# x and w turned by VectorE in 32x32 blocks and placed by DMA, in a two-layer graph network

## The chip, the cores and the metric

The kernel runs on one core of a Trainium2 chip, as one program. The metric is the device time of one execution in microseconds. Five engines work side by side, each through its own queue in order: TensorE (PE in the profile, its weight loads PEld), VectorE (DVE), ScalarE (ACT), GpSimd (POOL) and SyncE (SP), which here only issues DMAs. An instruction starts when those before it on its engine are through and the semaphores that it waits for have been raised.

## The reference

64 graphs of 256 nodes with 256 features each. Cut to what matters:

```python
# layer 0, for all graphs; d = 256
xc = transpose(x, (0, 2, 1))
h = relu(bn1(conv1d(xc, conv1_w, 0)))                # width 1
h = bn2(conv1d(h, conv2_w, 8))                       # width 17
x_conv = transpose(relu(h + xc), (0, 2, 1))
s = x @ w_se.T + b_se                                # 3 numbers a node
A = exp(-dist(s)) * adj
msg = relu(x @ w_msg.T + b_msg)
x_nmp = einsum('bnm,bmd->bnd', A, msg)
gi = concatenate([x_conv, x_nmp], -1) @ w_ih.T + b_ih
gh = x @ w_hh.T + b_hh
r, z = sigmoid(gi_r + gh_r), sigmoid(gi_z + gh_z)
out0 = (1 - z) * tanh(gi_n + r * gh_n) + z * x
x = layernorm(x + out0)
# layer 1
h = layernorm(x)
agg = einsum('bij,bjh->bih', adj, h)
x = layernorm(x + x + relu(agg @ W_rel + b_rel + h @ W_root))
```

The inputs besides `x` and `adj` are weights, biases and batch-norm statistics. All is float32.

## The kernel before

Features lie on partitions in layer 0 (a node's features run down the partitions, in C = 2 halves of 128), nodes lie on partitions in layer 1. So x has to be turned once at the start, and the result of layer 0, called w (twice the sum of x and the layer's output), once in the middle.

**Batches and pairs.** The width-17 convolution works on batches of 8 graphs (`conv`, 8 batches b = 0 to 7), all else on pairs of two graphs (`pair`, 32 pairs p = 0 to 31, four to a batch). The convolution is computed as products of polynomials: `split`, `merge` and `butterflies` are VectorE work on the tile XF, `products` has TensorE's matmuls with the transformed filters. These filters are computed once, stored to DRAM (w2m), and for batches after the first loaded in portions into the two halves of the tile cs (`load_w`, 768 KB each, two portions in flight). `conv1(b)` prepares a batch: for each two graphs it loads x (`fetch`), turns it by eight TensorE transposes through PSUM and two ScalarE copies into xTc (`turned`), stores xTc to DRAM (xt), multiplies by the width-1 filter and stores the result (hd), which the convolution loads later into XF. `pair(p)` loads xT from xt again.

**A pair** goes through: msg and the three numbers of s (`ps_msg`), the distances (`ps_sT`, `ps_dist`), A (AT times adjm), nmp; the sum of convolution and x (xc); the gates. For pairs 2 to 30 the gate products are done in seven instead of eight block products: differences of blocks are formed by VectorE in tx (of xT), tn (of nmp) and tc (of xc), and `product` multiplies them by sums of weight blocks in WB. A gate's sums leave the PSUM banks `ps_a`, `ps_b`, `ps_d` by `put` (ScalarE, into RG for r and the hidden part, into ZN for z and n) and `onto` (VectorE). Then five VectorE operations over 1024 columns and a tanh make w in the tile wT, features on partitions.

**norm, project, aggregate.** `norm` turns w: eight TensorE transposes per pair into two PSUM banks (`ps_wT`). For pairs 0 to 27 ScalarE copies each half of a bank to x1 and sums it on the way (`total`), then squares it with the mean taken off (into the part of HY that is free then), GpSimd makes the factors q and the shifts sh from the sums, and ScalarE normalizes x1 in place. For the last four pairs (`late`) VectorE takes the statistics directly from PSUM. `project` multiplies wT with both weight matrices of layer 1 (`ps_hy`), scales by q into HY; `aggregate` multiplies by the adjacency (`ps_agg`), adds, takes the maximum with zero and adds x1, sums, normalizes and stores to out.

**The order** is not the order of the code. Every operation is recorded with a due time (`prog.at(when, step)`; a pair's due is 143.0 + 60.5 p us, GATE_TIME is the planned length of a gate) and planned costs (`dur`, for a DMA 0.06 us on SyncE's queue and its bytes at 205 GB/s after 1.6 us), and `scheduled` builds each engine's queue from these, taking of the operations that are ready the one with the earliest due time. `prog.group()` makes one planned operation of several instructions. The built program keeps this order on each engine whatever the real times are. The eight PSUM banks are given out by the planner, at most 4 to the gates, 3 to the convolution, 6 to the rest. All DMAs but three small ones at the start (ScalarE's) go through SyncE's queue; in the built program they use eight semaphores in turn, so a DMA also waits for the one issued eight before it.

Of the kernel before, what the change touches and what calls it, by code (L numbers as in the profile page):

```python
# [15 lines left out]
AF = mybir.ActivationFunctionType  # L16
ALU = mybir.AluOpType

P = 128
# [31 lines left out]
LEAVES += [(U + 2, U + 3, PI / 2)]  # L51
NM = 3 * len(LEAVES) + 2
SR, LR = 32, 100
OB = 7
HQ = 2 * M * C * (M + 1)
XC_SLOTS = BG + 2
FIRST_GATES, PERIOD, GATE_TIME = 143.0, 60.5, 18.0
AHEAD_FROM, AHEAD_TO, W_DEEP = -20.0, 10.0, 2
CONV1_FROM, CONV1_TO, CONV_FROM, CONV_OUT, CONV_TO = -10.0, 120.0, -6.0, -70.0, -30.0
PAIR_LEAD, FILTER_LEAD, LOAD_AHEAD = 20.0, 15.0, 12.0  # L60
PLAIN, SUMS_FROM = (0, 1, B // 2 - 1), 2


# [199 lines left out]
class Engine:  # L263
# [4 lines left out]
    def __getattr__(self, method):  # L268
        program, name = self.program, self.name

        def call(*args, hold=(), need=(), lines_up=0, **named):
            line = sys._getframe(1 + lines_up).f_lineno
            outs = [v for v in (named.get("out"), named.get("accum_out"), named.get("out_")) if v is not None]
            outs += [] if "out" in named else [args[0]]
            ins = [v for v in list(args) + list(named.values()) if not any(v is o for o in outs)]
            if method == "matmul" and not named.get("start", True):
                ins.append(outs[0])

            def places(vs):
                return [v if isinstance(v, View) else dram_cells(v) for v in vs  # L280
                        if isinstance(v, View) or hasattr(v, "tensor")]
            n = max((v.size() for v in outs if isinstance(v, View)), default=0)
            moved = 0
            if method == "dma_start":
                v = outs[0] if isinstance(outs[0], View) else named["in_"]
                dur, moved = 0.06, v.size() * v.at.shape[0] * 4
            elif name == "tensor":
                turned = method == "transpose" or named.get("is_transpose")
                dur = 0.109 if turned else 2 * max(0.109, n * 0.8333e-3 + 0.0025)
            elif name == "vector":  # L290
                dur = 0.182 if method == "bn_aggr" else 0.147 + 1.044e-3 * (args[1].size() if method == "bn_stats" else n)
# [114 lines left out]
def gnn_two_layers(  # L406
# [373 lines left out]
    def conv1(b):  # L780
# [3 lines left out]
        XN = {}  # L784

        def fetch(g):
            if b > 0:
                XN[g] = xn_ahead[:, :4 * D].rearrange("p (j d) -> p j d", d=D)
            elif g >= 4:
# [4 lines left out]

        def turned(g):
            xn = XN[g]
            if b > 0 or g == 4:
                xTc = xTc_ahead
            elif g:
# [39 lines left out]
    def conv(b):  # L839
# [8 lines left out]
        if b == 0:  # L848
            run(other)
        sv, s8, s4 = {}, {}, {}  # L850
        todo = [(lambda k=k: products(b, 2 * k, S + 2 * k), merges(0, k, S, sv, b == 0)) for k in range(4)]
        todo += [(lambda k=k: products(b, 8 + 2 * k, S2 + 2 * k), merges(1, k, S2, s8, b == 0)) for k in range(2)]
        todo += [(lambda: products(b, 12, S2 + 4), merges(2, 0, S2 + 4, s4, b == 0)), (lambda: last_products(b), None)]
        vector = deque([other])
        share, spent = 61.0 / len(todo), 0.0
        for i, (make, after) in enumerate(todo):
# [80 lines left out]
    bhh = sb("bhh", [P, 3, C])  # L937
    half_r = sb("half_r", [P, C])
    half_z = sb("half_z", [P, C])
    sts = sb("sts", [P, 3 * LR + P])  # L940
    sts.base.fine = 0
    lr = sb("lr", [P, 2, N])
    prog.at(22.0, 0.001)
# [28 lines left out]
    store_w2(1)  # L972

    xTs = [sb(f"xT{i}", [P, C, 2, N], "ahead") for i in range(2)]
    msg = sb("msg", [P, 2, C, D], "ahead")
    AT = sb("AT", [P, 2, C, N], "ahead")
    adjm = sb("adjm", [P, 2, C, N], "ahead")
    nmp = sb("nmp", [P, C, 2, N], "ahead")

    first = conv(0)  # L980
    at4 = len(prog.ops)
# [3 lines left out]
    opened["work"] = first_closed  # L985
    WB = sb("WB", [P, 7, 3, 3, P], "work")
    tx = sb("tx", [P, 4, N], "work")
    tn = sb("tn", [P, 3, N], "work")
    tc_ = sb("tc", [P, 3, N], "work")
    RG = sb("RG", [P, 4, 2, N], "work")  # L990
    ZN = sb("ZN", [P, 4, 2, N], "work")
# [58 lines left out]
    def pair(p):  # L1050
# [10 lines left out]
        at = p % 2 * C * LR  # L1061
        st = sts[:, at:at + C * LR].rearrange("p (m e) -> p m e", m=C)

        def spot(m, g):
            o = at + m * LR + 2 * g * SR
            return sts[:, o:o + 2 * SR].rearrange("p (r e) -> p r e", r=2)[:, :, 0:3]
        idle = p < 2
        for g in range(2):
            for m in range(C):
# [5 lines left out]
                    if idle:  # L1075
                        PE.matmul(ps[:, :D + 4], ones[0:1, :], bms[0:1, :], start=False, stop=True)
                if idle:
                    A.copy(spot(m, g), ps[:, D:D + 3].unsqueeze(1).to_broadcast([P, 2, 3]))
                    A.activation(msg[:, g, m], ps[:, :D], AF.Relu)
                    continue  # L1080
                V.tensor_add(spot(m, g), ps[:, D:D + 3].unsqueeze(1).to_broadcast([P, 2, 3]),
                             bms[:, D:D + 3].unsqueeze(1).to_broadcast([P, 2, 3]))
                V.tensor_add(msg[:, g, m], ps[:, :D], bms[:, :D])
            if not idle:
                A.activation(msg[:, g], msg[:, g], AF.Relu)
        sq, ns = next(sqs), next(nss)
        s = st[:, :, :3 * SR].rearrange("p m (r e) -> p m r e", e=SR)[:, :, ::2, 0:3]
        G.tensor_mul(sq, s, s)
# [39 lines left out]
        A.activation(xc, xc, AF.Relu)  # L1128
        ins = (xT, nmp, xc)
        right = []  # L1130
        for v, t, when in zip(ins, (tx, tn, tc_), (due - 28, due - 10, due - 20)):
# [5 lines left out]
            t1, t2, t4 = (t[:, i, :] for i in range(3))  # L1137
            t3 = t[:, 3, :] if v is xT else b12
            V.tensor_sub(t1, b12, b11)
            V.tensor_sub(t2, b22, t1)  # L1140
            V.tensor_sub(t4, b21, t2)
            V.tensor_sub(t3, b22, b12)
            right.append((b11, b21, b22, t4, t1, t2, t3))

        def product(ps, i, second, start):
# [94 lines left out]
        def norm(gs):  # L1240
# [2 lines left out]
            js = slice(2 * gs[0], 2 * gs[-1] + 2)  # L1243
            total, squares, mv = next(totals), next(totals), next(mvs)
            source = {}
            for g in gs:
                ps = bank("ps_wT")
                with prog.group():
                    for m in range(C):
# [14 lines left out]
            else:  # L1264
# [4 lines left out]
            G.tensor_scalar(q[:, 0, js], var, part, 4 * EPS, ALU.mult, ALU.add)  # L1269
            G.tensor_scalar(q[:, 1, js], var, (1 + EPS) * part, 4 * EPS * EPS, ALU.mult, ALU.add)  # L1270
            G.tensor_tensor(q[:, :, js], q[:, :, js], mhalf.rearrange("p (a c) -> p a c", a=2)[:, :, js], ALU.pow)
            G.tensor_mul(sh[:, js], mean, q[:, 0, js])
            if late:
                G.tensor_scalar(sh[:, js], sh[:, js], -1.0, None, ALU.mult)
            for g, m, j in spots(gs):
                A.activation(x1[:, g, m, :], source[j], AF.Identity, bias=sh[:, j:j + 1], scale=q[:, 0, j:j + 1])
            return q

        def project(gs, q):
            prog.at(due + 2 * GATE_TIME + 8, 0.6)  # L1280
            for g, m, j in spots(gs):
                ps = bank("ps_hy")
                with prog.group():
                    for f in range(C):
                        PE.matmul(ps, wT[:, 2 * f + g, m * P:(m + 1) * P], wrr[:, f, :], start=(f == 0),  # L1285
                                  stop=(f == C - 1), hold=[HY[:, g, m]], need=[q[:, 1, j:j + 1]])
                stt(HY[:, g, m, :], ps, q[:, 1, j:j + 1], hrow)  # L1287

        def aggregate(gs):
            prog.at(due + 2 * GATE_TIME + 16, 0.4)  # L1290
            q, sh = next(q3s), next(shs)
            js = slice(2 * gs[0], 2 * gs[-1] + 2)
            total, squares, mv = next(totals), next(totals), next(mvs)
            for g in gs:
# [5 lines left out]
                                      start=(m == 0), stop=(m == C - 1))  # L1300
                y = HY[:, g, :, D:]
                V.tensor_add(y, y, ps.rearrange("p (m d) -> p m d", m=C))
                if late:
                    stt(y, y, 0.0, x1[:, g], op0=ALU.max, op1=ALU.add)
                for m in range(C):
                    j = 2 * g + m
                    if late:
                        stats(mv[:, j, :], y[:, m, :])
                    else:
                        V.scalar_tensor_tensor(y[:, m, :], y[:, m, :], 0.0, x1[:, g, m], op0=ALU.max, op1=ALU.add,  # L1310
                                               accum_out=total[:, j:j + 1])
            if late:
                mean, var, part = mv[:, js, 0], mv[:, js, 1], 1.0
            else:
# [5 lines left out]
            G.tensor_scalar(q[:, js], var, part, EPS / 4, ALU.mult, ALU.add)  # L1320
            G.tensor_tensor(q[:, js], q[:, js], mhalf[:, js], ALU.pow)
            G.tensor_mul(sh[:, js], mean, q[:, js])
            if late:
                G.tensor_scalar(sh[:, js], sh[:, js], -1.0, None, ALU.mult)
            for g in gs:
                y = HY[:, g, :, D:]
                for m in range(C):
# [120 lines left out]
```

## Time and profile before

| | us |
|---|---|
| median of 3 runs | 2087.59 |
| lowest, highest | 2084.59, 2087.82 |
| profiled execution | 2085.32 |
| span of the profiled execution (first to last instruction) | 2083.5 |
| mean granted TensorE clock | 0.994 |
| DMA queue of SyncE: packets, MB, share of the span of 16 engines | 207518, 238.92, 35.6% |

Busy time by stage, from stretches of the same execution:

| stretch, us | what | PE busy | DVE busy | ACT busy | DMA share |
|---|---|---|---|---|---|
| 143 to 385 | pairs 0 to 3 | 238.48 | 181.93 | 106.44 | 0.43 |
| 627 to 869 | four pairs in the middle | 241.75 | 206.60 | 123.16 | 0.37 |
| 1353 to 1595 | four pairs later | 241.83 | 207.54 | 121.15 | 0.36 |
| 1900 to 2020 | pairs without convolution beside them | 117.96 | 71.09 | 53.40 | 0.13 |
| 2060 to 2084 | the end | 10.91 | 9.11 | 3.09 | 0.06 |

From 143 us on the pairs follow each other about 60 us apart, and TensorE is busy nearly all of it. The profile counts matmuls in records: a product of float32 is two records, a transpose one. The page's part on DMA issues gives the median time from issue to landing:

```profile
cs<-w2m SPq DMA_DIRECT2D x105, 768.0 KB, 4.8
adjm<-in_adjT_dram SPq DMA_DIRECT2D x64, 256.0 KB, 2.8
xT<-xt SPq DMA_DIRECT2D x32, 512.0 KB, 3.7
out_dram<-HY SPq DMA_DIRECT2D x64, 256.0 KB, 2.1
```

SyncE's own operations carry the time that the engine needs to issue a DMA, without its transfer.

### The profile page before, as it was taken

How to read it: one execution, taken by the hardware profiler on the slowest of the kernel's cores; microseconds unless marked ns; L12 is line 12 of the kernel's file. 1: busy time of each engine (PE TensorE's matmuls, PEld its weight loads, DVE VectorE, ACT ScalarE, POOL GpSimd, SP SyncE). 2: the span in 40 equal slices, each digit the busy share in tenths (PEclk: the TensorE clock that was granted, in tenths of full speed). 3: DMA queues.
4: the chain of work that ended last, by engine and by line, in shares of the span. 5: the costliest groups of instructions: out<-in, count | busy, mean ns of one | idle time of the engine just before them, and what ended most of it. 6: DMA issues, size and time to landing. Idle time of an engine off the chain costs nothing.

```text
span 2083.5 us, 28847 instructions
## 1 busy us (share of the span) xinstructions
PE 2048.0 (98%) x10492; PEld 1664.2 (80%) x10492; DVE 1685.8 (81%) x3028; ACT 1018.1 (49%) x2216; POOL 317.2 (15%) x555
## 2 busy tenths in 40 slices
PE   9989999999999999999999999999999999999996
PEld 6868779778887788878888788877888779887775
DVE  7983898899868998789868998689887899875644
ACT  7443433754447544564436544464445544365432
POOL 4100210122111201111101121112011220011101
PEclk9989999999999999999999999999999999999999
DMA  7734363334423244224433245232442225211100
GB/s 211 262 98 144 124 208 112 118 102 141 161 81 120 92 160 141 94 92 141 165 107 113 72 139 170 96 112 91 159 138 83 76 74 161 75 50 53 41 21 31
DMA packets 208201, 241.19 MB, mean 116 GB/s; under 512 B 23749, under 2 KB 192700, under 8 KB 208060
## 3 DMA queue, kind: packets, MB, share of 16 engines
q1 hardware_dynamic: 207518, 238.92, 35.6%
q8 instruction: 83, 1.36, 0.3%
q14 instruction: 58, 0.48, 0.1%
q10 hardware_dynamic: 542, 0.43, 0.1%
HBM read 177.85 MB, written 61.47 MB: 115 GB/s over the span
## 4 chain that ended last, share of the span: by engine, by line
PE 94%; DVE 4%; issue 1%; ACT 0%; POOL 0%; ACTq 0%; POOLq 0%; DVEq 0%
PE ps_a L1155 21%; PE ps_k L703 16%; PE ps_d L1155 11%; PE ps_hy L1285 11%; PE ps_msg L1073 5%; PE ps_agg L1299 5%; PE ps_c L828 5%; PE ps_b L1155 5%; PE ps_g L1155 5%; PE ps_nmp L1121 4%; PE ps_w L561 2%; PE ps_wT L1252 1%; PE ps_xTc L807 1%; PE ps_dist L1107 1%; DVE RG L1230 1%
## 5 line engine op out<-in xcount | busy, mean ns | idle before, releaser
L703 PEld LDWEIGHTS ps_k<-XF,cs 128*128 128x128 f32 x2632 | 313.2, 192 | 13.0 <-issue 6.6
L703 PE MATMUL ps_k<-XF,cs 128*128 128x128 f32 x2632 | 315.4, 275 | 0.0
L1285 PE MATMUL ps_hy<-wrr,wT 128*128 128x512 f32 x512 | 226.8, 595 | 0.0
L1285 PEld LDWEIGHTS ps_hy<-wrr,wT 128*128 128x128 f32 x512 | 96.6, 191 | 107.0 <-issue 102.1
L1169 ACT ACTIVATE RG<-ps_a,bhh 128x512 f32<-128x512 f32 x116 | 79.5, 686 | 191.0 <-PE ps_a L1155 129.4
L1155 PE MATMUL ps_a<-tx,WB 128*128 128x256 f32 x522 | 156.7, 382 | 0.0
L1167 ACT COPY ZN<-ps_a 128x512 f32<-128x512 f32 x116 | 67.6, 583 | 156.5 <-PE ps_a L1155 156.2
L1287 DVE SCALAR_TENSOR_TENSOR HY<-ps_hy,q,hrow 128x512 f32<-128x512 f32 x128 | 95.8, 749 | 55.8 <-PE ps_hy L1285 41.1
L675 DVE TENSOR_TENSOR XF<-XF 128x512 f32<-128x512 f32 (+3 forms) x128 | 126.4, 1010 | 5.3 <-ACT XF L756 3.0
L1073 PE MATMUL ps_msg<-wms,xT 128*128 128x260 f32 x512 | 124.7, 384 | 0.0
L1299 PE MATMUL ps_agg<-HY,adja 128*128 128x256 f32 x512 | 119.1, 380 | 4.0 <-issue 3.5
L1121 PE MATMUL ps_nmp<-AT,msg 128*128 128x256 f32 x512 | 118.8, 380 | 3.0 <-DVE AT L1114 3.0
L1299 PEld LDWEIGHTS ps_agg<-HY,adja 128*128 128x128 f32 x512 | 96.3, 190 | 31.3 <-issue 16.1
L1073 PEld LDWEIGHTS ps_msg<-wms,xT 128*128 128x128 f32 x512 | 95.3, 190 | 19.1 <-issue 5.8
L1121 PEld LDWEIGHTS ps_nmp<-AT,msg 128*128 128x128 f32 x512 | 95.4, 190 | 18.8 <-DVE AT L1114 4.2
L828 PE MATMUL ps_c<-xTc,w 128*128 128x512 f32 x232 | 107.7, 594 | 0.5 <-ACT xTc L808 0.5
L1155 PEld LDWEIGHTS ps_a<-tx,WB 128*128 128x128 f32 x522 | 95.1, 191 | 14.0 <-issue 1.5
L1155 PE MATMUL ps_a<-tc,WB 128*128 128x256 f32 x348 | 103.8, 380 | 0.0
L1155 PE MATMUL ps_a<-xc,WB 128*128 128x256 f32 x348 | 103.6, 379 | 0.0
L1155 PE MATMUL ps_a<-tn,WB 128*128 128x256 f32 x348 | 103.5, 379 | 0.0
L1155 PE MATMUL ps_a<-nmp,WB 128*128 128x256 f32 x348 | 103.5, 379 | 0.0
L1265 POOL TENSOR_SCALAR total<-total 128x4 f32<-128x4 f32 x28 | 15.5, 552 | 544.9 <-ACT x L1261 544.9
(213 smaller groups left out, 4642.7 us busy)
## 6 DMA issues: line engine op xcount, KB each, us to landing
cs<-w2m SPq DMA_DIRECT2D x105, 768.0 KB, 4.8
adjm<-in_adjT_dram SPq DMA_DIRECT2D x64, 256.0 KB, 2.8
xT<-xt SPq DMA_DIRECT2D x32, 512.0 KB, 3.7
adja<-in_adjT_dram SPq DMA_DIRECT2D x64, 256.0 KB, 2.7
out_dram<-HY SPq DMA_DIRECT2D x64, 256.0 KB, 2.1
hd<-xn SPq DMA_DIRECT2D x28, 544.0 KB, 3.2
XF<-hd SPq DMA_DIRECT2D x28, 544.0 KB, 4.0
xt<-xTc SPq DMA_DIRECT2D x29, 512.0 KB, 4.0
```

The lines of the kernel that those rows point to most:

```text
L561: PE.matmul(ps[:, :NM * OB], TT[i][:, a, :], taps, start=True, stop=True)
L675: (V.tensor_add if add else V.tensor_sub)(sl(o, n), sl(a, n), sl(b, n))
L703: PE.matmul(ps[:, o * P:(o + 1) * P], w(m, c)[:, o * P:(o + 1) * P], X[:, slot, c * P:(c + 1) * P], start=first and o == 0 and c == 0, sto ...
L828: PE.matmul(ps, w1[:, c, o * P:(o + 1) * P], xTc[:, c, :], start=(c == 0), stop=(c == C - 1), hold=[h[:, :, o]])
L1073: PE.matmul(ps[:, :D + 4], xT[:, c, g, m * P:(m + 1) * P], wms[:, c, :], start=(c == 0), stop=(c == C - 1 and not idle), hold=[msg[:, g, m]])
L1121: PE.matmul(ps[:, d * N:(d + 1) * N], msg[:, g, m, d * P:(d + 1) * P], AT[:, g, m, :], start=(m == 0), stop=(m == C - 1), hold=[nmp[:, :, g]])
L1155: PE.matmul(ps[:, h * N:(h + 1) * N], block[:, s, gate, :], right[s][at], start=start and h == 0 and j == 0, stop=j == len(sources) - 1, s ...
L1167: A.copy(o, ps)
L1169: A.activation(o, ps, AF.Identity, bias=bhh[:, 2, f:f + 1])
L1285: PE.matmul(ps, wT[:, 2 * f + g, m * P:(m + 1) * P], wrr[:, f, :], start=(f == 0), stop=(f == C - 1), hold=[HY[:, g, m]], need=[q[:, 1, j: ...
L1287: stt(HY[:, g, m, :], ps, q[:, 1, j:j + 1], hrow)
L1299: PE.matmul(ps[:, n_ * D:(n_ + 1) * D], adja[:, g, m, n_ * P:(n_ + 1) * P], HY[:, g, m, :D], start=(m == 0), stop=(m == C - 1))
```

## The change

For batches 3 to 7 (`TURN_FROM`) x is loaded in runs of 32 floats by 16 DMAs for two graphs, each to 32 partitions, so that 32x32 blocks lie where their turned ones belong; one VectorE operation turns all blocks into xTc. For pairs 2 to 27 (`W_FROM`, not `late`) w is turned likewise: VectorE turns the blocks of wT into the part of ZN that n has left free, and 32 DMAs of 128 runs of 128 bytes carry the blocks to their places in x1, where ScalarE sums them (into the scratch part of HY). The transposes of TensorE and the evictions from PSUM for these are gone. `project` and `aggregate` of these pairs are due 15 us later (`W_LAG`); the planner counts the bytes of grouped DMAs 2.5 times (`SMALL_RUNS`).

Small operations are joined: the bias is added to msg and s at once over 260 columns, and s is copied to its places by ScalarE; the differences for tx and for nmp (whose tile now holds the differences too, tn is gone) partly two at once; `merge` joint in every batch; in `aggregate` the maximum and sum with x1 for both halves at once, with the sums taken by ScalarE. For late pairs some small operations on statistics go from GpSimd to VectorE, and a multiplication by -1 is joined. In the last pair the products of `project` no longer wait for q.

```diff
-FIRST_GATES, PERIOD, GATE_TIME = 143.0, 60.5, 18.0
+FIRST_GATES, PERIOD, GATE_TIME = 143.0, 60.5, 17.0
+SMALL_RUNS, TURN_FROM = 2.5, 3
+W_FROM, W_LAG = 2, 15.0
...
                 dur, moved = 0.06, v.size() * v.at.shape[0] * 4
+                if program.joined is not None:
+                    moved *= SMALL_RUNS
...
         def fetch(g):
+            if b >= TURN_FROM:
+                XN[g] = xn_ahead[:, :4 * D]
+                blocks = XN[g].rearrange("p (c g b i) -> p g c b i", c=C, g=2, i=SQ)
+                with prog.group():
+                    for a in range(P // SQ):
+                        for k in range(2):
+                            for c in range(C):
+                                at = c * P + a * SQ
+                                SP.dma_start(out=blocks[a * SQ:(a + 1) * SQ, k, c], in_=x[b * BG + g + k][
+                                    :, at:at + SQ].rearrange("(b j) i -> j b i", j=SQ))
+                return
...
         def turned(g):
             xn = XN[g]
+            if b >= TURN_FROM:
+                V.transpose(xTc_ahead.rearrange("p c n -> p (c n)"), xn)
+                SP.dma_start(out=xt_dram[(b * BG + g) // 2], in_=xTc_ahead)
+                return xTc_ahead
...
                 if idle:
-                    A.copy(spot(m, g), ps[:, D:D + 3].unsqueeze(1).to_broadcast([P, 2, 3]))
-                    A.activation(msg[:, g, m], ps[:, :D], AF.Relu)
+                    A.copy(msg[:, g, m], ps[:, :D + 4])
                     continue
-                V.tensor_add(spot(m, g), ps[:, D:D + 3].unsqueeze(1).to_broadcast([P, 2, 3]),
-                             bms[:, D:D + 3].unsqueeze(1).to_broadcast([P, 2, 3]))
-                V.tensor_add(msg[:, g, m], ps[:, :D], bms[:, :D])
-            if not idle:
-                A.activation(msg[:, g], msg[:, g], AF.Relu)
+                V.tensor_add(msg[:, g, m], ps[:, :D + 4], bms)
+        for m in range(C):
+            A.copy(places(m), msg[:, :, m, D:D + 3].unsqueeze(2).to_broadcast([P, 2, 2, 3]))
+        for g in range(2):
+            A.activation(msg[:, g, :, :D], msg[:, g, :, :D], AF.Relu)
...
-            for g in gs:
+            if not late and p >= W_FROM:
+                blocks = ZN[:, :, 1, :]
+                V.transpose(blocks.rearrange("p j (c n) -> p j c n", c=C),
+                            wT.rearrange("p (c g) (m n) -> p (g m) c n", c=C, m=C))
+                with prog.group():
+                    for a in range(P // SQ):
+                        for b in range(P // SQ):
+                            for c in range(C):
+                                SP.dma_start(
+                                    out=x1[b * SQ:(b + 1) * SQ].rearrange("j g m d -> j (g m) d")[
+                                        :, :, c * P + a * SQ:c * P + (a + 1) * SQ],
+                                    in_=blocks[a * SQ:(a + 1) * SQ, :, c * P + b * SQ:c * P + (b + 1) * SQ])
+                for g, m, j in spots(gs):
+                    source[j] = x1[:, g, m, :]
+                    A.activation(HY[:, g, m, :D], x1[:, g, m, :], AF.Copy, accum_out=total[:, j:j + 1])
+            for g in gs if late or p < W_FROM else ():
...
-            prog.at(due + 2 * GATE_TIME + 8, 0.6)
+            prog.at(due + 2 * GATE_TIME + 8 + (0.0 if late or p < W_FROM else W_LAG), 0.6)
...
-                                  stop=(f == C - 1), hold=[HY[:, g, m]], need=[q[:, 1, j:j + 1]])
+                                  stop=(f == C - 1), hold=[HY[:, g, m]], need=[] if apart else [q[:, 1, j:j + 1]])
...
-                if late:
-                    stt(y, y, 0.0, x1[:, g], op0=ALU.max, op1=ALU.add)
+                stt(y, y, 0.0, x1[:, g], op0=ALU.max, op1=ALU.add)
...
-                        V.scalar_tensor_tensor(y[:, m, :], y[:, m, :], 0.0, x1[:, g, m], op0=ALU.max, op1=ALU.add,
-                                               accum_out=total[:, j:j + 1])
+                        A.activation(HY[:, g, m, :D], y[:, m, :], AF.Copy, accum_out=total[:, j:j + 1])
```

More of the change, by code (lines that the diff above doesn't have):

```diff
@@ L53 @@
 SR, LR = 32, 100
+SQ = 32
 OB = 7
@@ L850, in conv @@
         sv, s8, s4 = {}, {}, {}
-        todo = [(lambda k=k: products(b, 2 * k, S + 2 * k), merges(0, k, S, sv, b == 0)) for k in range(4)]
-        todo += [(lambda k=k: products(b, 8 + 2 * k, S2 + 2 * k), merges(1, k, S2, s8, b == 0)) for k in range(2)]
-        todo += [(lambda: products(b, 12, S2 + 4), merges(2, 0, S2 + 4, s4, b == 0)), (lambda: last_products(b), None)]
+        todo = [(lambda k=k: products(b, 2 * k, S + 2 * k), merges(0, k, S, sv, True)) for k in range(4)]
+        todo += [(lambda k=k: products(b, 8 + 2 * k, S2 + 2 * k), merges(1, k, S2, s8, True)) for k in range(2)]
+        todo += [(lambda: products(b, 12, S2 + 4), merges(2, 0, S2 + 4, s4, True)), (lambda: last_products(b), None)]
         vector = deque([other])
@@ L939, in gnn_two_layers @@
     half_z = sb("half_z", [P, C])
-    sts = sb("sts", [P, 3 * LR + P])
+    sts = sb("sts", [P, LR + P + 4])
     sts.base.fine = 0
@@ L974, in gnn_two_layers @@
     xTs = [sb(f"xT{i}", [P, C, 2, N], "ahead") for i in range(2)]
-    msg = sb("msg", [P, 2, C, D], "ahead")
+    msg = sb("msg", [P, 2, C, D + 4], "ahead")
     AT = sb("AT", [P, 2, C, N], "ahead")
     adjm = sb("adjm", [P, 2, C, N], "ahead")
-    nmp = sb("nmp", [P, C, 2, N], "ahead")
+    nmps = sb("nmp", [P, 7, N], "ahead")
+    nmp = nmps[:, 1:5].rearrange("p (c g) n -> p c g n", c=C)
     first = conv(0)
@@ L987, in gnn_two_layers @@
     tx = sb("tx", [P, 4, N], "work")
-    tn = sb("tn", [P, 3, N], "work")
     tc_ = sb("tc", [P, 3, N], "work")
@@ L1060, in pair, with places @@
         prog.at(due - 62, 0.6)
-        at = p % 2 * C * LR
+        at = p % 2 * 4
         st = sts[:, at:at + C * LR].rearrange("p (m e) -> p m e", m=C)
-        def spot(m, g):
-            o = at + m * LR + 2 * g * SR
-            return sts[:, o:o + 2 * SR].rearrange("p (r e) -> p r e", r=2)[:, :, 0:3]
+        def places(m):
+            o = at + m * LR
+            return sts[:, o:o + 4 * SR].rearrange("p (g r e) -> p g r e", g=2, r=2)[:, :, :, 0:3]
         idle = p < 2
@@ L1130, in pair @@
         right = []
-        for v, t, when in zip(ins, (tx, tn, tc_), (due - 28, due - 10, due - 20)):
+        for v, t, when in zip(ins, (tx, nmps, tc_), (due - 28, due - 10, due - 20)):
             prog.at(when, 0.3)
@@ L1136, in pair @@
                 continue
-            t1, t2, t4 = (t[:, i, :] for i in range(3))
+            t1, t2, t4 = (t[:, i, :] for i in ((0, 5, 6) if v is nmp else range(3)))
             t3 = t[:, 3, :] if v is xT else b12
-            V.tensor_sub(t1, b12, b11)
+            if v is xT:
+                V.tensor_sub(t[:, 0::3], v[:, :, 1, :], v[:, 0])
+            elif v is nmp:
+                V.tensor_sub(t[:, 0:3:2], t[:, 2:5:2], t[:, 1:3])
+            else:
+                V.tensor_sub(t1, b12, b11)
             V.tensor_sub(t2, b22, t1)
             V.tensor_sub(t4, b21, t2)
-            V.tensor_sub(t3, b22, b12)
+            if v is xc:
+                V.tensor_sub(t3, b22, b12)
             right.append((b11, b21, b22, t4, t1, t2, t3))
@@ L1268, in norm @@
                 mean, var, part = total[:, js], squares[:, js], 1.0 / D
-            G.tensor_scalar(q[:, 0, js], var, part, 4 * EPS, ALU.mult, ALU.add)
-            G.tensor_scalar(q[:, 1, js], var, (1 + EPS) * part, 4 * EPS * EPS, ALU.mult, ALU.add)
+            small = V if late else G
+            small.tensor_scalar(q[:, 0, js], var, part, 4 * EPS, ALU.mult, ALU.add)
+            small.tensor_scalar(q[:, 1, js], var, (1 + EPS) * part, 4 * EPS * EPS, ALU.mult, ALU.add)
             G.tensor_tensor(q[:, :, js], q[:, :, js], mhalf.rearrange("p (a c) -> p a c", a=2)[:, :, js], ALU.pow)
-            G.tensor_mul(sh[:, js], mean, q[:, 0, js])
             if late:
-                G.tensor_scalar(sh[:, js], sh[:, js], -1.0, None, ALU.mult)
+                stt(sh[:, js], mean, -1.0, q[:, 0, js], op1=ALU.mult)
+            else:
+                G.tensor_mul(sh[:, js], mean, q[:, 0, js])
             for g, m, j in spots(gs):
@@ L1285, in project @@
                         PE.matmul(ps, wT[:, 2 * f + g, m * P:(m + 1) * P], wrr[:, f, :], start=(f == 0),
-                                  stop=(f == C - 1), hold=[HY[:, g, m]], need=[q[:, 1, j:j + 1]])
+                                  stop=(f == C - 1), hold=[HY[:, g, m]], need=[] if apart else [q[:, 1, j:j + 1]])
                 stt(HY[:, g, m, :], ps, q[:, 1, j:j + 1], hrow)
         def aggregate(gs):
-            prog.at(due + 2 * GATE_TIME + 16, 0.4)
+            prog.at(due + 2 * GATE_TIME + 16 + (0.0 if late or p < W_FROM else W_LAG), 0.4)
             q, sh = next(q3s), next(shs)
@@ L1319, in aggregate @@
                 mean, var, part = total[:, js], squares[:, js], 1.0 / D
-            G.tensor_scalar(q[:, js], var, part, EPS / 4, ALU.mult, ALU.add)
+            (V if late else G).tensor_scalar(q[:, js], var, part, EPS / 4, ALU.mult, ALU.add)
             G.tensor_tensor(q[:, js], q[:, js], mhalf[:, js], ALU.pow)
-            G.tensor_mul(sh[:, js], mean, q[:, js])
             if late:
-                G.tensor_scalar(sh[:, js], sh[:, js], -1.0, None, ALU.mult)
+                stt(sh[:, js], mean, -1.0, q[:, js], op1=ALU.mult)
+            else:
+                G.tensor_mul(sh[:, js], mean, q[:, js])
             for g in gs:
```

## The prediction

> **What bounds the kernel now.** I read the page's engine table first, then the groups by shape, then TensorE's timeline, then SyncE's own timeline. Columns of a group: line, engine, operation, tiles, shape, count | busy us, mean ns | idle before it.
>
> ```profile
> PE 2048.0 (98%) x10492; PEld 1664.2 (80%) x10492; DVE 1685.8 (81%) x3028; ACT 1018.1 (49%) x2216; POOL 317.2 (15%) x555
> PE 94%; DVE 4%; issue 1%; ACT 0%; POOL 0%; ACTq 0%; POOLq 0%; DVEq 0%
> L1252 PE MATMUL ps_wT<-ident,wT 128*128 128x128 f32 x256 | 35.5, 281 | 10.4 <-DVE wT L1231 10.4
> L807 PE MATMUL ps_xTc<-ident,xn 128*128 128x128 f32 x224 | 31.8, 273 | 0.0
> L1231 DVE SCALAR_TENSOR_TENSOR wT<-ZN,RG 128x1024 f32<-128x1024 f32 x28 | 34.3, 1225 | 1.0
> ```
>
> TensorE is busy 98% of the span and 94% of the chain of waits, so a TensorE instruction taken away is worth its pace, as long as nothing makes TensorE wait. The pace is the distance of starts in its timeline (start, length, engine, line, count), since the 273 ns of one matmul include an overlapped tail:
>
> ```profile
> 609.26 1.06 PE L1252 MATMUL ps_wT<-ident,wT 128*128 128x128 f32 x8 [0.17 <-DVE wT L1231]
> 610.16 0.60 PE L807 MATMUL ps_xTc<-ident,xn 128*128 128x128 f32 x4
> 610.60 0.60 PE L1155 MATMUL ps_d<-tx,WB 128*128 128x256 f32 x2
> 611.03 0.59 PE L1155 MATMUL ps_d<-tc,WB 128*128 128x256 f32 x2
> ```
>
> Eight transposes take 0.90 us: 0.112 us each. One 256-column product (two records) takes 0.43.
>
> **What comes off.** The built order of the changed kernel has 5203 TensorE instructions instead of 5571: 26 pairs x 8 of w and 5 batches x 4 x 8 of x, 368 in all. 368 x 0.112 = 41 us. In the last pair, four small GpSimd operations on statistics go to VectorE and two of them are dropped (rows of 0.31 to 0.46 us against 0.15 or so); this chain stands bare at the end, about -2 us. Gain in sight: 43 us.
>
> **VectorE and ScalarE.** 46 block turns of 128x1024 come to VectorE. No row shows one; I take 1.22 us, the row of any other 1024-element operation there (L1231); between half and twice that, the chain below moves by -0.6 to +1.2 us. Against 46 x 1.22 = 56 us stand the joined operations: 120 spot additions (L1081, 161 ns) and 112 half-size sums with accumulation (L1310, 423 + 82 ns, now 56 of some 0.69 us) leave, two merges or subtractions become one. Counted out with the rows by size, VectorE's total stays within 10 us. ScalarE gets 112 sums (0.49 us each), loses 40 evictions (0.587): about +50 us on 49%. Neither is near a bound; both are priced nothing on the path, and the cover is their idle time.
>
> **The DMAs, which are the price.** w is no longer evicted from PSUM: 32 DMAs of 16 KB per pair bring the blocks from ZN to x1, and 16 per two graphs bring x. All go through SyncE's one queue. Its rows (a small transfer each in the first fence; the second has two in a row in mid-kernel):
>
> ```profile
> 24.64 0.43 SPq L956 DMA_DIRECT2D hrow<-in_rows_dram  x1
> 25.12 0.43 SPq L957 DMA_DIRECT2D gb<-in_rows_dram  x1
> 25.59 0.51 SPq L958 DMA_DIRECT2D bih<-in_rows_dram  x1
> ```
>
> ```profile
> 142.28 0.39 SPq L793 DMA_DIRECT2D xn<-in_x_dram  x1
> 142.73 0.49 SPq L842 DMA_DIRECT2D XF<-hd  x1
> ```
>
> The issue takes about the same for 2 KB (gb) as for 544 KB (XF): 0.34 to 0.54, and starts lie 0.45 to 0.48 apart. The shortest row is 0.319 (XF, min of 28). I take 0.45; ends 0.33 and 0.54. A train of 32 is then 14.4 us, with 16 of x 21.6. The planner in the kernel counts 0.06 an issue and, with the new factor of 2.5 on bytes, 6.4 + 1.6 = 8.0 us to the landing. I take the landing of the last at 2.1 (least row: out_dram): 16.5 in place of 8.0, so every train lands 8.5 us later than the order of all engines was laid out for.
>
> Could the transfer itself be slower than its issue? Two stretches (the last two columns are the DMA engines' busy share and GB/s):
>
> ```profile
> 60.00:100.00 40.00, 40.00 (x277) 34.69 (x275) 36.69 (x57) 16.81 (x38) 1.87 (x1) 1.00 0.83 274
> 131.00:133.00 2.00, 2.00 (x10) 1.26 (x11) 2.00 (x4) 0.75 (x4) 0.12 (x1) 1.00 0.92 267
> ```
>
> In the second the 512-byte runs of WB load: 512 / (267 / 0.92 / 16) = 28 ns a packet. A train has 4096 / 16 = 256 packets an engine: 7 us at that price, below 14.4. The trend to the 1 KB packets of the first (w2m; 1024 / (274 / 0.83 / 16) = 50 ns) would make 128 bytes about 13 ns, 3 us. So issue decides.
>
> The Trainium skill speaks against the change here: "DMA: Bandwidth & Descriptors", Specifications, says that below 512 bytes a transfer costs a read-modify-write. Taken as two passes of the 28 ns row, an estimate by that page would be 56 ns a packet and 14.3 us a train, equal to the issue; no row here shows 128-byte runs. The same page (Issuing engines are not separate DMA queues) calls the time to initiate a DMA usually small beside the DMA; the rows above show 0.4 us beside 16 KB, where it is the larger part.
>
> **Where the lateness arrives.** From the last gate product of a pair to the end of the wait: onto 0.69, two updates 2.44, two tanh 1.44, three updates 3.66, turn 1.22 = 9.45; train and landing 16.5; then ScalarE, in order, reads x1 four times (4 x 0.49 = 2.0) and only behind these stands the put (0.65) of the next pair's gate product. Sum 28.6. While ScalarE waits, TensorE works on, until its order reaches an instruction that needs a ScalarE result from behind the reads. I summed TensorE's work between these two points in the built order by the paces above, for the 26 pairs. In 16 it is short: 18.6, 19.5, 20.3, 20.3, 20.8, 20.8, 20.8, 20.9, 22.1, 24.3, 25.2, 25.5, 25.8 and three of 26.4, together 364.1; the other ten have 29.9 to 44.8 and hide it. (The least, pair 27: 31 gate products, 8 of msg, 4 of nmp, 43 x 0.43 = 18.6.) Wait: 16 x 28.6 - 364.1 = 93.5 us. With the planner's 8.0 the chain is 20.1 and the same count leaves 2 us.
>
> Behind the trains in SyncE's queue stand the loads of cs (4.7 us to land) for the convolution. Chain 9.45 + 14.4 + 4.7 = 28.6, or 35.8 where the 16 of x go first. TensorE's work up to the product that needs the load: 26.1, 23.7, 23.0, 28.4, 28.9, 22.4, 20.0 (against 28.6) and 34.2, 31.7 (against 35.8). The shortfalls come to 26 us, the 20.0 counted only by what exceeds the wait on ScalarE in its pair. The xT loads have 50 us and more: nothing. The changed GATE_TIME and W_LAG are in the orders counted.
>
> Sum: 93.5 + 26 - 43 = +76.5 us. The profiled execution took 2085.3 (span 2083.5), the median of the runs is 2087.6: 2087.6 + 76.5 = 2164.
>
> **The ends.** At 0.33 an issue the chain is 24.8: shortfalls 39 + 5, -43: +1, 2089. At 0.54 it is 31.5: 141 + 51 - 43 = +149, 2237. This is the likeliest case's own range.
>
> **Rivals.** (1) The trains are as cheap as planned: 32-partition transfers issue in 0.2 us or less, chain 20.1, 2 us of waits: 2087.6 - 43 + 2 = 2047. For it: no row has 32 partitions, and issue rows do vary. Against: rows with 2 KB and 0.8 KB are no shorter than those with 768 KB. It decides below some 0.33 us an issue, where the waits equal the 43. (2) Packets decide: at the 50 ns of the 1 KB row a train of w and one of x are 256 x 50 ns each, 25.6 us of the 60.5 of a pair on top of some 21.5 in use (35.6%), and trains queue behind loads: 3 us more on the chain of 16 pairs, 48, and on the 9 loads, 27: 2164 + 75 = 2239. Against: the 28 ns row. (3) The waits are there but partly taken up by work that the count calls fixed, since ScalarE's puts catch up with 49% load: half of 120 us remains, 2087.6 + 60 - 43 = 2105.
>
> **Chances.** Likeliest case 0.60, packets 0.10, half absorbed 0.15, cheap trains 0.15. A change of 0.2%, 4 us, is about what can be told from none. Faster: the cheap trains less a little, 0.13; same 0.04 (from the low end of the likeliest and the half-absorbed case); slower 0.83. Range 2080 to 2238: from just below the low end to packets' price, leaving out most of rival 1 and the tail above.
>
> **What would show it.** Right: SyncE's rows of L1279 start 0.42 to 0.48 apart; ScalarE's L1285 waits for DMA some 8 us in most pairs; TensorE stands idle before ps_a (L1180) for ScalarE and before ps_k (L708) for cs, together near 120 us; its busy sum falls by 41. Wrong: rows of L1279 under 0.3 us, or TensorE still 98% busy. If L1279 lands 5 us or more after its issue, packets decide.

## The result, and the profile after

The changed kernel takes 2400.6 us (median of 4 runs, 2395.3 to 2405.4) against 2087.6 before: 1.1508 times as long, 95% interval 1.1493 to 1.1522. The forecast had the direction and the place, and a quarter of the size: +313 us instead of +76. The profiled execution has a span of 2398.7 us (before 2083.5).

From the page of the changed kernel, the engine table, the chain that ended last by engine, and three groups (line, engine, operation, tiles, shape, count | busy us, mean ns | idle before it and what ended that):

```profile
PE 2084.8 (87%) x10124; PEld 1671.5 (70%) x10124; DVE 1710.3 (71%) x2613; ACT 1044.5 (44%) x2460; POOL 270.8 (11%) x520
PE 60%; SPq 22%; DVE 8%; DMA 5%; ACT 3%; issue 2%; POOL 0%; ACTq 0%; POOLq 0%; DVEq 0%
L1285 ACT ACTIVATE HY<-x 128x256 f32<-128x256 f32 x104 | 41.9, 403 | 354.2 <-DMA x<-ZN 354.2
L1273 DVE STREAM_TRANSPOSE ZN<-wT 128x1024 f32<-128x1024 f32 x26 | 32.4, 1245 | 0.9
L1180 PE MATMUL ps_a<-tx,WB 128*128 128x256 f32 x522 | 169.0, 407 | 118.6 <-ACT RG L1194 68.3 <-ACT ZN L1192 50.1
```

TensorE has 368 records fewer and yet is busy 36.8 us longer; it stands idle 313.9 us (2398.7 - 2084.8) instead of 35.5. These two differences, 36.8 + 278.4, are the whole 315.2 us of span. SyncE's queue, which had no share of the chain before, has 22% of it.

One train of w in the middle of the run, in SyncE's timeline, and the summary of the line (duration in ns: least, median, most):

```profile
941.59 21.26 SPq L1279 DMA_DIRECT2D x<-ZN  x32
L1279 SPq DMA_DIRECT2D x<-ZN x832: 585/599/1830, 363.9 to 2202.2; - x167
```

32 issues in 21.26 us are 0.665 each. What ScalarE and TensorE do meanwhile, each in its own timeline (start, length, engine, line):

```profile
948.72 0.69 ACT L1194 ACTIVATE RG<-ps_a,bhh 128x512 f32<-128x512 f32 x1 [3.64 <-PE ps_a L1180]
964.12 0.42 ACT L1285 ACTIVATE HY<-x 128x256 f32<-128x256 f32 x1 [14.71 <-DMA x<-ZN]
...
965.74 0.56 ACT L1192 COPY ZN<-ps_a 128x512 f32<-128x512 f32 x1
```

```profile
958.49 0.59 PE L1180 MATMUL ps_b<-nmp,WB 128*128 128x256 f32 x2
966.35 1.22 PE L1180 MATMUL ps_a<-tx,WB 128*128 128x256 f32 x2 [7.26 <-ACT ZN L1192]
967.37 1.06 PE L1180 MATMUL ps_a<-tc,WB 128*128 128x256 f32 x2
968.22 1.06 PE L1180 MATMUL ps_a<-nmp,WB 128*128 128x256 f32 x2
```

ScalarE waits 14.7 us for the blocks at the head of its queue; behind its four reads stands the put of a gate's sum (965.74), and TensorE, which had worked on until 959, needs the result of that put and waits 7.3 us. Then something is seen that the forecast had no term for: the next products (two to a row) come with rows 0.85 us apart instead of 0.43. The stretches around it (the columns before the last two: granted clock):

```profile
940.00:958.00 18.00, 18.00 (x85) 15.80 (x84) 16.80 (x30) 2.06 (x3) 0.00 (x0) 1.00 0.21 46
958.00:966.00 8.00, 1.08 (x6) 0.60 (x4) 1.46 (x3) 1.88 (x9) 0.09 (x1) 0.90 0.35 81
966.00:972.00 6.00, 5.65 (x13) 4.20 (x14) 3.10 (x5) 5.47 (x16) 3.43 (x7) 0.56 0.50 198
972.00:1000.00 28.00, 26.50 (x107) 18.30 (x105) 19.41 (x28) 24.04 (x55) 3.09 (x9) 1.00 0.40 131
```

In the 6 us after a wait of 7 us the granted clock is 0.56 on average. Over the run it is 0.933 (0.994 before), and the 2007 us that TensorE's work should take (2048.0 - 41) became 2084.8: 78 us more. The trace's clock records show how much of this is the clock: TensorE was busy for 153 us at the halved clock (17 us before), and half of the difference is 68 us. What the other 10 us are was not traced. The Trainium skill has this in "TensorE: Matmul & The Clock Gate", Part 1: the clock is halved after an idle window of some 3.4 us and comes back after a busy one of the same length. The trace agrees: each of TensorE's 34 waits of 3.6 us or more brought a halved clock, which ended 2.8 to 9.0 us after TensorE went on.

### The profile page after: what moved, and what is told of

Its sections match the earlier page's. It is cut to its first block, busy times and chain, and to the rows that moved or that the text cites. A ratio compares the mean times of both kernels' runs of the same rounds, so it can differ in the third digit from the quotient of the medians.

```text
span 2398.7 us, 29158 instructions
## 1 busy us (share of the span) xinstructions
PE 2084.8 (87%) x10124; PEld 1671.5 (70%) x10124; DVE 1710.3 (71%) x2613; ACT 1044.5 (44%) x2460; POOL 270.8 (11%) x520
## 4 chain that ended last, share of the span: by engine, by line
PE 60%; SPq 22%; DVE 8%; DMA 5%; ACT 3%; issue 2%; POOL 0%; ACTq 0%; POOLq 0%; DVEq 0%
SPq L1279 20%; PE ps_a L1180 12%; PE ps_k L708 11%; PE ps_hy L1327 9%; PE ps_d L1180 7%; PE ps_agg L1341 4%; PE ps_g L1180 4%; PE ps_nmp L1140 3%; PE ps_c L848 3%; DMA cs<-w2m 2%; SPq L800 2%; PE ps_w L566 2%; PE ps_b L1180 2%; DMA x<-ZN 1%; PE ps_msg L1093 1%
## 5 line engine op out<-in xcount | busy, mean ns | idle before, releaser
L708 PE MATMUL ps_k<-XF,cs 128*128 128x128 f32 x2632 | 330.3, 284 | 86.3 <-DMA cs<-w2m 60.9
L708 PEld LDWEIGHTS ps_k<-XF,cs 128*128 128x128 f32 x2632 | 326.6, 200 | 111.2 <-issue 55.4
L1180 PE MATMUL ps_a<-tx,WB 128*128 128x256 f32 x522 | 169.0, 407 | 118.6 <-ACT RG L1194 68.3
L1180 PE MATMUL ps_a<-nmp,WB 128*128 128x256 f32 x696 | 217.3, 395 | 0.0
L1285 ACT ACTIVATE HY<-x 128x256 f32<-128x256 f32 x104 | 41.9, 403 | 354.2 <-DMA x<-ZN 354.2
L1198 DVE TENSOR_TENSOR RG<-RG,ps_d 128x512 f32<-128x512 f32 x58 | 39.6, 683 | 178.4 <-ACT RG L1194 163.5
L1180 PEld LDWEIGHTS ps_a<-nmp,WB 128*128 128x128 f32 x696 | 139.3, 200 | 21.4 <-ACT nmp L1142 0.2
L1093 PE MATMUL ps_msg<-wms,xT 128*128 128x260 f32 x512 | 134.8, 386 | 10.8 <-DMA xT<-xt 10.8
L1305 POOL TENSOR_SCALAR total<-total 128x4 f32<-128x4 f32 x28 | 6.4, 229 | 962.2 <-ACT HY L1285 951.5
L1180 PE MATMUL ps_a<-tc,WB 128*128 128x256 f32 x348 | 112.3, 407 | 0.0
```

The lines of the kernel that those rows point to most:

```text
L708: PE.matmul(ps[:, o * P:(o + 1) * P], w(m, c)[:, o * P:(o + 1) * P], X[:, slot, c * P:(c + 1) * P], start=first and o == 0 and c == 0, sto ...
L1093: PE.matmul(ps[:, :D + 4], xT[:, c, g, m * P:(m + 1) * P], wms[:, c, :], start=(c == 0), stop=(c == C - 1 and not idle), hold=[msg[:, g, m]])
L1180: PE.matmul(ps[:, h * N:(h + 1) * N], block[:, s, gate, :], right[s][at], start=start and h == 0 and j == 0, stop=j == len(sources) - 1, s ...
```

## The experiments

All ratios are to the kernel before, with 95% intervals.

| run | what | median us | ratio | clock |
|---|---|---|---|---|
| after | the change | 2400.6 | 1.1508 [1.1493, 1.1522] | 0.933 |
| e1 | joins alone | 2080.1 | 0.9972 [0.9961, 0.9983] | 0.995 |
| e2 | joins and x | 2065.1 | 0.9896 [0.9881, 0.9911] | 0.994 |
| e3 | joins and w | 2412.3 | 1.1559 [1.1542, 1.1576] | 0.934 |
| e4 | the change, true price in the plan | 2198.0 | 1.0535 [1.0518, 1.0553] | 0.968 |
| e5 | half as many DMAs | 2115.2 | 1.0136 [1.0121, 1.0151] | 0.985 |
| e6 | e2 and w's trains for nobody | 2186.8 | 1.0476 [1.0458, 1.0493] | 0.974 |
| e7 | half as many, true price | 2102.4 | 1.0074 [1.0059, 1.0089] | 0.984 |
| e8 | as e7, w through DRAM | 2097.8 | 1.0052 [1.0035, 1.0070] | 0.992 |
| e9 | as e7, two queues | 2088.7 | 1.0006 [0.9997, 1.0015] | 0.990 |
| e10 | e2, half as many DMAs | 2064.6 | 0.9901 [0.9886, 0.9915] | 0.996 |
| e11 | e10, x of batches two and three too | 2059.8 | 0.9874 [0.9858, 0.9891] | 0.994 |

**The parts alone (e1, e2, e3).** Each is the changed kernel with a constant or two set so that the condition never holds:

```diff
 # e1: both;  e2: the second;  e3: the first
-SMALL_RUNS, TURN_FROM = 2.5, 3
-W_FROM, W_LAG = 2, 15.0
+SMALL_RUNS, TURN_FROM = 2.5, 99
+W_FROM, W_LAG = 99, 15.0
```

> Joined operations and new planner constants alone; x and w are turned by TensorE as before. Theory (the train of w's block DMAs is the loss): 2075 to 2100 us, within some 0.6% of before, TensorE's granted clock 0.99 and idle time about 35 us as before. Rival (the joins, the sums moved to ScalarE or the shorter planned gate disturb the order): 2200 us or more.

> x of batches four to eight turned by VectorE, w by TensorE, joins kept. Theory: the x trains (16 issues, 8.6 us) are waited for by nothing near, so 160 transposes x 0.112 = 18 us come off: 2060 to 2085 us. Rival (any train of small DMAs holds up SyncE's loads of the filters): 320 of the 1152 small DMAs, so about a quarter of the 313 us, 2150 us or more.

> w of pairs 2 to 27 turned by VectorE, x by TensorE, joins kept. Theory: all of the loss stays, 2380 to 2430 us (the 18 us of x's transposes are back); ScalarE waits for the blocks some 350 us in 26 waits and TensorE's clock is near 0.93. Rival (x and w trains together fill SyncE's queue): clearly less than after, 2300 us or lower.

The joins give 6 us, the turn of x another 15 (expected 18), and w has all the loss: 2412.3 - 2080.1 = 332 us. All three rivals fall. In e3 ScalarE waits 377.5 us in 26 waits, at a clock of 0.934. So small DMAs are not a loss in themselves: with 20 trains of 16 for x a gain of 15 of the 18 us is left, while 26 trains of 32 for w cost 332 us. The two kinds differ in length (8.6 and 21.3 us) as well as in what waits for them; e5 and e6 take this apart.

**What an issue costs (p1).** A kernel of trains alone, issued back to back.

> Only trains of DMAs, nothing of the computation (zeros and raw blocks go to the output). What does one issue cost by its form? Theory A (fixed price of an issue, longer where both ends lie in SBUF): L36 (32 partitions x 4 runs, SBUF to SBUF) about 0.60 us, L39 (twice the runs) the same, L41 and L44 (from DRAM) 0.45, L46 and L49 (one run a partition, SBUF to SBUF) near 0.60 too. Theory B (price by descriptors): L39 twice L36, L46 a quarter of it. Theory C (0.45 alone, 0.60 only because the queue is busy with other loads): all forms 0.45 or less here. Landing of a train's last about 1.8 us after its issue.

SyncE's lines there (duration in ns: least, median, most; L36 is w's form, L39 the same with twice the runs, L41 and L44 load from DRAM as x does, L46 has one run of 512 bytes a partition, L49 one of 128 bytes on all 128 partitions, L51 eight of 64 bytes on all 128, L56 stores to DRAM), then ScalarE's queue, which issued w's form too, and a stretch in which both queues did (last columns: clock, DMA share, GB/s):

```profile
L36 SPq DMA_DIRECT2D t<-src x32: 599/614/787, 4.4 to 24.9; - x32
L39 SPq DMA_DIRECT2D t<-src x16: 599/608/610, 25.6 to 35.4; - x16
L41 SPq DMA_DIRECT2D t<-in_x_dram x32: 312/430/597, 1.2 to 49.3; - x32
L44 SPq DMA_DIRECT2D t<-in_x_dram x16: 430/449/450, 49.7 to 57.1; - x16
L46 SPq DMA_DIRECT2D t<-src x32: 570/588/590, 57.6 to 77.2; - x32
L49 SPq DMA_DIRECT2D t<-src x32: 592/599/601, 77.9 to 97.8; - x32
L51 SPq DMA_DIRECT2D t<-src x8: 648/676/677, 98.4 to 103.5; - x8
L56 SPq DMA_DIRECT2D out_dram<-src x32: 428/430/662, 104.2 to 119.1; - x32
```

```profile
4.37 20.87 ACTq L54 DMA_DIRECT2D t<-src  x32
```

```profile
6.00:24.00 18.00, 0.00 (x0) 0.00 (x0) 1.00 0.32 50
```

Theory A holds, nearly: an issue costs 0.59 to 0.61 us where both ends lie in SBUF and 0.43 to 0.45 where one lies in DRAM, with little regard to partitions, runs or bytes. Only the form with the most runs (L51, 1024 runs of 64 bytes) takes more, 0.68; it was not among the forms expected. Starts lie some 0.05 us further apart than an issue takes. L39, L46 and L49 had no other load beside them, so the price is not one of a busy queue. SyncE and ScalarE issued w's form at the same time, 32 in 21.17 and 20.87 us, which is the pace of L39 alone (16 in 10.39). And packets are cheap: 128 / (50 / 0.32 / 16) = 13 ns each. The trace's own records of 128-byte packets have a mean of 12 ns here, for L36 as for the stores to DRAM of L56, and of 12.6 in the changed kernel.

**Half as many DMAs (e5).** The blocks get a contiguous tile, so that both halves c go in one DMA (the loads of x are joined likewise, from 16 to 8; not shown):

```diff
-                blocks = ZN[:, :, 1, :]
+                blocks = ZN[:, 0:2].rearrange("p a h n -> p (a h) n")
...
-                            for c in range(C):
-                                SP.dma_start(
-                                    out=x1[b * SQ:(b + 1) * SQ].rearrange("j g m d -> j (g m) d")[
-                                        :, :, c * P + a * SQ:c * P + (a + 1) * SQ],
+                            SP.dma_start(
+                                out=x1[b * SQ:(b + 1) * SQ].rearrange("j g m (c e) -> j (g m c) e", c=C)[
+                                    :, :, a * SQ:(a + 1) * SQ],
```

> The same bytes in the same 128-byte runs, but in half as many DMAs (16 of 32 KB for w from a block tile that is contiguous, 8 of 64 KB for x). Theory (time goes by issued DMA): trains of 16 x 0.6 to 0.7 = 10 to 11 us, ScalarE's wait falls from 13.6 us a pair to 3 or less, time 2080 to 2150 us. Rival (time goes by packet or by descriptor of 128 bytes): each DMA takes twice as long to issue, 1.2 us or more, trains stay 21 us, time stays 2380 to 2420 us.

A train in SyncE's timeline and ScalarE's wait in all (us, times, longest):

```profile
363.63 10.55 SPq L1277 DMA_DIRECT2D x<-ZN  x16
```

```profile
ACT HY L1284 <- DMA x<-ZN: 89.4, 19, 8.8
```

The same 4096 runs in half the issues take half the time, ScalarE's wait falls from 354 to 89 us (3.4 a pair, a little more than expected), and 285 of the 313 us are gone, the lost clock included (0.985). Joining the loads of x has no part in this, as e10 shows. So the number of issues is the cause, not the runs.

**The price in the plan (e4).** The same instructions in another order:

```diff
-                    moved *= SMALL_RUNS
+                    dur = 0.54 if named["in_"].__class__ is not View else 0.665
...
-            dma = max(dma, now + 1.6) + op.moved / 205e3
+            if len(op.calls) > 1:
+                dma = max(dma, now + op.dur + 1.8)
+            else:
+                dma = max(dma, now + 1.6) + op.moved / 205e3
```

> The changed kernel with another order only: the planner counts 0.665 us (w) and 0.54 us (x) for each grouped DMA on SyncE's queue and the landing 1.8 us after the last, instead of 0.06 and 2.5 times the bytes. Same instructions. Theory (the order was laid out for trains of 8 us; with 23 known, work stands in front of the waits): most of the waits go, 2130 to 2220 us. Rival (SyncE's queue itself, or the distance from w to x1, has no room however the order is): above 2320 us.

ScalarE's wait for the blocks is nearly gone:

```profile
ACT HY L1288 <- DMA x<-ZN: 10.2, 8, 3.1
```

TensorE's waits for the filters fall from 60.9 to 6.1 us as well. 203 of the 313 us come back by order alone. Nearly none of the other 110 are waits for blocks: TensorE's idle time there is 134 us in many waits of 1 to 6 us (for gate puts, distances, nmp), and the clock is 0.968. How they come about was not followed further.

**Trains that nobody waits for (e6).** w is turned by TensorE; the trains go from a constant to spare places.

```diff
+                SP.dma_start(out=(spare, ones)[c][b * SQ:(b + 1) * SQ].rearrange("j (q d) -> j q d", q=4),
+                             in_=wrr[a * SQ:(a + 1) * SQ].rearrange("p c (h d) -> p (c h) d", h=2)[
+                                 :, :, c * P + b * SQ:c * P + (b + 1) * SQ], need=[wT])
...
-            for g in gs if late or p < W_FROM else ():
+            for g in gs:
```

> As e2 (x by VectorE, w by TensorE), but SyncE still issues the 26 trains of 32 block DMAs, from a constant into spare places that nobody reads, so no engine waits for them; only the loads that stand behind them in SyncE's queue come later. Nothing of the output changes. Theory (most of the loss is ScalarE waiting for the blocks with the gates' sums behind it; the shortfalls at 0.665 us an issue are about 210 us there and 90 us at the loads): 2065 plus at most 90 us of late loads plus some lost clock, 2110 to 2200 us. Rival (SyncE's queue held for 21 us and the transfers themselves are the loss): above 2300 us. Rival (the loads cost nothing): below 2085 us.

+122 us over e2: TensorE stands idle 86 us longer (at most 90 were expected) and is busy 35 us longer. By the clock records it was busy at the halved clock for 61 us more than in e2, which explains 31 of the 35. The longest of TensorE's waits are those for the filters' loads behind the trains:

```profile
PE ps_k L708 <- DMA cs<-w2m: 36.4, 8, 9.8
```

VectorE also waits 83 us for loads of x behind the trains (0.7 us in e2). So of the 336 us between e2 and the change, trains that nobody waits for make about 122, lost clock included (0.974); the held queue and the transfers themselves are not told apart here. The rest, about 214, and the 23 us that w's transposes would have saved, is left for those who wait for the blocks. This is a difference, not a measurement: one wait can hide in another, and e6 also lacks the later due time of `project` and `aggregate`.

**Shorter trains with the true price (e7, e8, e9).** e7 is e5 with e4's planner. e8 carries w by 4 stores to DRAM and 4 loads; e9 gives half of the 16 DMAs to ScalarE's queue:

```diff
+                for queue, part in ((SP, (0, 1)), (A, (2, 3))):
...
-                            SP.dma_start(
+                            queue.dma_start(
```

> e5 and e4 together: half as many DMAs, and the planner counts 0.65 us (w) and 0.49 us (x) an issue. Theory (the loss is lateness against the order, and both the length of a train and its price in the plan make it): 2070 to 2110 us, ScalarE's wait for the blocks under 30 us in all, clock 0.98 or more. Rival (the plan does not matter once trains are short): as e5, 2105 to 2120 us.

> As e7, but w goes through DRAM: 4 stores in runs of 128 bytes and 4 loads in runs of 512 bytes instead of 16 DMAs inside SBUF. By the trains issued alone, one side in DRAM costs 0.48 us an issue instead of 0.66: 4 x 0.48 + 1.5 + 4 x 0.48 + 2.0 = 7.3 us instead of 12.5. Theory: as e7 or up to 20 us less, 2060 to 2105 us. Rival (reading back what was just written to DRAM is slow): above e7 by 20 us or more.

> As e7, with half of w's 16 DMAs issued by ScalarE. The trains issued alone ran on both queues at once at full pace, so w takes 8 x 0.65 + 2.0 = 7.2 us instead of 12.4. Theory: 2050 to 2085 us, perhaps below e2 (2065), since the 23 us of w's transposes come off TensorE and little waiting is left. Rival (two queues share one issuer, or ScalarE's 5 us a pair cost as much as they save): as e7 or slower.

e7 came in its range for the time, but ScalarE still waited 51.5 us (expected under 30). e8 is 5 us below e7, in its range, but the intervals overlap and the way is not as short as its sum: stores and loads landed 3.3 and 3.0 us after their issue (taken: 1.5 and 2.0), and ScalarE waited 108 us for the loads. e9 missed its range by 4 us: ScalarE's reads wait only 22 us, but it now issues 208 DMAs itself, 0.63 us each, 130 us in all. Still w by VectorE only draws level with the kernel before, 24 us behind e10 that turns w on TensorE. TensorE's idle time is 65 us in e9's profiled execution and 33.5 in e2's; what makes up the difference wasn't taken apart.

**The best version (e10, e11).** e10 is e2 with e5's loads of x; e11 also turns x of batches two and three (b = 1 and 2, `TURN_FROM = 1`) with the true price.

> As e2, but 8 DMAs instead of 16 for two graphs of x. Theory (nothing waits for a train of x, so its length is free): as e2, 2060 to 2070 us. Rival (the 8.6 us that a train of 16 holds SyncE's queue still cost something at the loads behind it): 10 us or more below e2.

> As e10, with x of batches two and three turned by VectorE too and the planner counting 0.49 us an issue: 64 transposes fewer, 64 x 0.112 = 7 us. Theory: 2053 to 2068 us. Rival (in the first batches VectorE or the loads are fuller and the turns come late): 2070 us or more.

e10 equals e2 (2064.6 and 2065.1): the trains of x may take about 8 us instead of 5 at no cost, since nobody waits near their end. That this has a limit, e6 shows with 26 trains of 21 us. e11 is another 5 us faster (expected: 7), has TensorE busy 98% and is the fastest of all:

```profile
PE 2021.9 (98%) x10268; PEld 1640.4 (80%) x10268; DVE 1686.1 (82%) x2595; ACT 1040.6 (51%) x2444; POOL 298.1 (14%) x520
```

## Why the prediction was wrong in size

- *What comes off, 43 us.* Right for TensorE: e1 has 10492 records and 2043.8 us busy, e11 224 transposes fewer and 2021.9. (224 x 0.112 = 25; measured 22.) Of the joins, priced at nothing but the end's 2 us, 6 came.
- *VectorE and ScalarE, nothing on the path.* The turn was right: 1.245 us (taken: 1.22). The totals were not: VectorE's busy time rose by 24.5 us (1685.8 to 1710.3; "within 10"), ScalarE's by 26 ("about +50"; the two terms printed for it give 31). Neither engine came near a bound. But VectorE waited 37 us, in seven waits, for loads of x behind w's trains, which the sum doesn't have.
- *The issue, 0.45 us, ends 0.33 and 0.54.* This step failed. All rows it was read from have one end in DRAM, and the trains of w run inside SBUF: 0.665. In the forecast's own sum this one price turns the 119.5 us of waits into 301, 181 of the 237 us that the forecast fell short. For x, from DRAM, three trains of 16 issues took 7.99, 8.16 and 8.62 us, 0.50 to 0.54 an issue, near the upper end. The landing, 2.1, was 1.8.
- *Where the lateness arrives.* Right as to the two places, less so as to their sizes: with 0.665 in the same sum the chain is 35.5 instead of 28.6, the 26 covers fall short by 211 us (204 of them in the sixteen listed) and the loads of cs by 90. Together 301; TensorE's idle time rose by 278. TensorE's longest waits by what ended them:

```profile
PE ps_a L1180 <- ACT RG L1194: 68.3, 7, 13.3
PE ps_k L708 <- DMA cs<-w2m: 60.9, 8, 9.8
PE ps_a L1180 <- ACT ZN L1192: 50.1, 7, 10.2
PE ps_d L1180 <- DVE RG L1198: 39.1, 4, 12.4
PE ps_a L1180 <- ACT xc L1147: 19.0, 6, 4.7
PE ps_k L708 <- DVE XF L680: 13.8, 1, 13.8
PE ps_k L708 <- DVE ZN L1198: 11.5, 1, 11.5
PE ps_msg L1093 <- DMA xT<-xt: 10.8, 3, 4.4
```

  The first, third and fourth are the gates' sums behind ScalarE, 157 us where the sum has 211; the second is the filters, 61 where it has 90. The other 60 us arrived where the forecast had nothing, most of it at xc, at VectorE's work before the products of the convolution and at the loads of xT, late three times. So the total agrees better than its parts.
- *The clock.* This term was missing from the sum: of the 78 us that TensorE's work took longer, a quarter on top of the waits, the clock records account for 68. The shortfalls in the sum were 2 to 10 us each; that a wait of this length is paid again in slower products wasn't asked.
- *Rivals.* Cheap trains: wrong, no issue in the changed kernel takes less than 0.31 us, and none of w's less than 0.585. Packets: wrong, 13 ns (the estimate from the two load rows was 13). The Trainium skill gives a read-modify-write for less than 512 bytes, "DMA: Bandwidth & Descriptors", Specifications; the 56 ns that the forecast estimated from it do not show, neither inside SBUF nor in p1's stores to DRAM. The 0.4 us "beside 16 KB" in the forecast had no row of 16 KB behind it; p1 has them, at 0.43 to 0.61. Half absorbed: wrong, 278 of 301 us arrived as idle time, if not all where expected.
- *The range* ended at 2238 because both its ends were rows of other forms. About a tenth of the 500 issue rows of the kernel before are longer than its 0.54; but none of them has both ends in SBUF, so no row there could give w's price.

With 0.665 and the 78 us, both taken from the result, the same sum is 2087.6 + 301 - 43 + 78 = 2424 against 2400.6. It is no forecast, and its waits are 23 us more than TensorE's idle time rose by.

## What to carry to other kernels

Price a DMA by its issue when it is small: one that moves 16 or 32 KB inside SBUF held its queue for 0.66 us, so 32 of them were 21 us, and merging dimensions until half as many were left (e5) was worth 285 us. Moving work off the bounding engine helped here only where nothing stood close behind the detour: x, for whose blocks VectorE waited 0.7 us in all (e2), gained; w, with 19 to 26 us of TensorE's work as cover in most pairs, lost. In an order fixed beforehand, a wrong price for one step is paid by whatever the plan has put behind it in an in-order queue, here the gates behind ScalarE's reads, so put measured prices into the planner first.

## What had not been expected of the hardware

An issue cost 0.59 to 0.61 us with both ends in SBUF, for 32 or 128 partitions and runs of 128 or 512 bytes, and 0.68 for eight runs of 64 bytes on 128 partitions; it cost 0.43 to 0.45 in the trains with one end in DRAM (p1). Two issuing engines did this side by side at the pace of one alone (32 in 20.87 and 21.17 us). A packet of 128 bytes took 12 to 13 ns, a quarter of one of 1 KB (50 ns by the forecast's row of w2m). And TensorE's clock was 0.56 in the 6 us after a wait of 7.3 us; over the run, 278 us more of standing idle came with 68 us that TensorE lost by working at the halved clock.
